# Four banks for transposes, attention as columns, and another split of the single rows in a gather, attention and pooling kernel

## The chip, the cores and the metric

The kernel runs on one NeuronCore of a Trainium2 chip. The metric is the device time of one execution in microseconds (us). The kernel before takes 13519.97 us, the median of 3 runs (13496.62 to 13551.33). One more execution was profiled; the numbers of the profile are its own.

The engines of a core work side by side, each through its own queue of instructions in order: TensorE (PE, with PEld for its weight loads), VectorE (DVE), ScalarE (ACT), GpSimd (POOL) and SyncE (SP, here only a queue for DMAs). They wait for each other by semaphores. PE writes its results into PSUM, which has eight banks of 2 KB in each partition.

## The reference

The inputs are 16384 users with 69 fields each (an index into a table of 100001 rows of 96 float32), and one label index each. In short:

```python
u   = emb[batch_user]                        # 16384 x 69 x 96
ql  = emb[batch_label[:, 0]]                 # 16384 x 96
z   = concatenate([q, u, q - u, q * u])      # q is ql for every field
h   = dice(z @ W1 + b1)                      # 64 wide
att = (h @ W2 + b2) @ W3 + b3                # one number per user and field
pre = where(batch_user < ITEM_NUM, u * att, 0)
pooled = einsum('gf,bfe->bge', window, pre)  # 69 fields into 10 groups
x   = concatenate([pooled, ql])              # 1056 wide
h   = dice(bn(x @ Wf1 + bf1))                # 200
h   = dice(bn(h @ Wf2 + bf2))                # 80
out = h @ Wf3 + bf3                          # 1
```

`dice(x)` is `(alpha * (1 - p) + p) * x` with `p = sigmoid(bn(x))`. The 1.13 million rows of the gather, each of 384 bytes, are the bulk of the data. W1 is split so that `z @ W1` becomes `u @ (W1u - W1qu) + (q * u) @ Wp` and a part that depends on q alone.

## The kernel before, in words

**Tiling.** The batch is cut into 32 blocks of 512 users. A block has 69 chunks of 512 rows: 64 main chunks hold 8 users with their first 64 fields, and 5 tail chunks hold one of the last five fields for all 512 users. Main chunks are pooled by matmuls with window weights; tail chunks go, scaled by their attention, straight into the first layer of the top network with weights prepared for them (`V`). `chunk_of` (L64) numbers the chunks; in all blocks but the last one the five tail chunks come at the end of a block. A step handles two chunks, so there are 1104 steps (`NPAIR`).

**The way of a step.** `fetch` (L361) gathers: each chunk is four tiles of 128 rows, and one `indirect_dma_start` on POOL fetches one tile into the buffer `u` (L268). PE turns each tile into the PSUM tile `ptr`, and DVE copies `ptr` to `uT` (L378) and multiplies it by q into `quT` (L381). `ptr` has two banks. Two steps later `hidden` (L391) computes `ph` from `uT` and `quT` (L401, L405), and ACT computes the sigmoid `y` (L407). A step after that `product` forms the gated value on DVE (L414, L415). `attend_rows` does the attention of four steps at once: PE multiplies the 32-column weights `v2` with y, 32 output rows for each step (`prow`, L421), ACT copies these to the row tile `row` (L423), and a step later `turn_band` transposes it (`patt`, L438), so that each field's attention stands in a partition of its own. `weigh` (L448) makes from it the pooling weights `rw` of four steps. Nine steps after the fetch (`POOL_LAG`) `pool_sums` multiplies `u` by `rw` into one of three sets of `acc` (all three in one bank), and a step later `pool_copy` copies the set into `pooled` on DVE (L489). `u` has 17 buffers, and a gather into a buffer waits until the sums that read it are done.

**Single rows.** Of some chunks the fourth tile is not gathered by POOL. Its 128 rows are fetched one by one by plain DMAs from SP's or ACT's queue (`Singles`, L303), each with an address that the queue has loaded into registers, into a ring of buffers. SP does this for one tile in every 10 steps (109 tiles, 4 buffers), ACT for one in every 8 (136 tiles, 3 buffers), 16 rows in each step, between its own sigmoids. PE waits for these rows on a semaphore of their own.

**The rest.** At a block's end, eight quarter pieces of the top network's first layer (`top1`), then `top2` and `top3`, follow one per step. At a block's start `head_gather` fetches the rows of the labels, `head_turn` transposes them and `head_rows` computes q's part of the hidden layer. The last block has an order of its own, in which the top network runs for quarters of the block.

**What sets the order.** The order on each engine is written out: `plan` holds a list of pieces for each step, and they are emitted step by step under a manual schedule. In the order of a step stand: attention (every fourth step), tail attention, `hidden`, the single rows of ACT, `pool_sums`, `product`, `pool_copy`, `fetch`, `weigh`. The waits between engines are put in by the framework from the tiles that the instructions share; PSUM is guarded by bank.

Of the kernel before, what the change touches and what calls it, by code (L numbers as in the profile page):

```python
# [11 lines left out]
F32 = mybir.dt.float32  # L12
I32 = mybir.dt.int32
# [5 lines left out]
P = 128  # L19
# [21 lines left out]
POOL_LAG = 9  # L41
# [5 lines left out]
CLOSE = 8  # L47

# [3 lines left out]
SP_CHUNKS = [2 * (10 * s + 8) + 1 for s in range(109)]  # L52
SP_RING = 4
ACT_CHUNKS = [2 * (8 * s + 11) for s in range(136)]
ACT_RING = 3
ACT_ROWS = 16
# [6 lines left out]

def chunk_of(c):  # L64

    n, k = divmod(c, NCH)
    if n == NBLK - 1 and k >= EARLY:
        k = NMAIN + k - EARLY if k < EARLY + NTAIL else k - NTAIL
    return n, k
# [47 lines left out]
def rec_kernel(  # L117
# [132 lines left out]
    ps_tr = ctx.enter_context(tc.tile_pool(name="ps_tr", bufs=2, space=PSUM))  # L250
    ps_h = ctx.enter_context(tc.tile_pool(name="ps_h", bufs=2, space=PSUM))
    ps_x = ctx.enter_context(tc.tile_pool(name="ps_x", bufs=2, space=PSUM))
    ps_acc = ctx.enter_context(tc.tile_pool(name="ps_acc", bufs=1, space=PSUM))
    acc = ps_acc.tile([E, 3, 2, NS, G], F32, tag="acc", name="acc")
    ps_m = ctx.enter_context(tc.tile_pool(name="ps_m", bufs=1, space=PSUM))


# [9 lines left out]
    def gather(table, dst, index):  # L267
        nc.gpsimd.indirect_dma_start(  # L268
            out=dst,
            out_offset=None,  # L270
            in_=table,
            in_offset=bass.IndirectOffsetOnAxis(ap=index, axis=0),
        )
# [42 lines left out]

    def single(c, t):
        return places.get(c) if t == SLOT else None
# [5 lines left out]
    def read_rows(op, out, u, c, t, other, **how):  # L324

        at = single(c, t)
        ins = op(out, ring[:, at[0]].bitcast(F32) if at else u[:, 4 * (c % 2) + t, :], other, **how)  # L327
        if at:
            tc.declare_no_dep(ins.ins, group=f"ring{at[0]}", reason="waited for by semaphore")

# [13 lines left out]
    def head_rows(n):  # L344

        for h in range(2):
# [14 lines left out]
    def fetch(i, between=None):  # L361
# [4 lines left out]
        for j in range(2):  # L366
# [3 lines left out]
            ptr = ps_tr.tile([E, 512], F32, tag="tr", name=f"ptr{i}_{j}")  # L370
            for t in range(4):
                if single(2 * i + j, t):
                    wait_for_single(2 * i + j, t)
                else:
                    gather(rows, u[:, 4 * j + t, :], ids[n][:, 4 * k + t : 4 * k + t + 1])
                read_rows(nc.tensor.transpose, ptr[:, t * P : (t + 1) * P], u, 2 * i + j, t, ident)
# [40 lines left out]
    def attend_rows(b, n):  # L417

        pr = ps_x.tile([P, 512], F32, tag="x", name=f"prow{b}")[0 : 32 * n]
        for k in range(n):  # L420
            nc.tensor.matmul(pr[32 * k : 32 * (k + 1), :], v2, ys[b + k], start=True, stop=True)  # L421
        row = rpool.tile([P, 512], F32, tag="row", name=f"row{b}")[0 : 32 * n]
        nc.scalar.copy(row, pr)  # L423
        bands[b] = row
# [8 lines left out]
    def turn_band(b, n):  # L433

        row = bands.pop(b)
        pt = ps_x.tile([P, 4, n, 32], F32, tag="x", name=f"patt{b}")
        for t in range(4):
            nc.tensor.transpose(  # L438
                pt[:, t].rearrange("p k j -> p (k j)"), row[:, t * P : (t + 1) * P], ident[0 : 32 * n, 0 : 32 * n]
            )  # L440
        turned[b] = pt

    def weigh(b, n):

        pt = turned.pop(b)
# [14 lines left out]
    def pool_sums(i):  # L460
# [6 lines left out]
        pa = acc[:, i % 3]  # L467
# [12 lines left out]
        accs[i] = pa, todo  # L480

# [26 lines left out]
    def top1(n, cols, h, part, p1):  # L508

        if part == 0:  # L510

            banks, tag = (ps_h, "h") if n == NBLK - 1 and cols.start >= BLK // 2 and h == 1 else (ps_m, "m")
# [14 lines left out]
    def top2(n, cols):  # L527
        x2 = xpool.tile([D2, BLK], F32, tag="x2", name=f"x2_{n}_{cols.start}")[:, cols]
        g2 = xpool.tile([DH, BLK], F32, tag="g1", name=f"g2_{n}_{cols.start}")[0:D2, cols]
        p2 = ps_m.tile([D2, BLK], F32, tag="m", name=f"p2_{n}_{cols.start}")[:, cols]  # L530
# [5 lines left out]
    def top3(n, cols, x2):  # L536
        k0, k1 = cols.start // P, cols.stop // P
        p3 = ps_m.tile([P, k1 - k0], F32, tag="m", name=f"p3_{n}_{cols.start}")
# [4 lines left out]
    def store(n):  # L543

        p4 = ps_x.tile([n, P], F32, tag="x", name="p4")
# [5 lines left out]
    def top3_last(x2):  # L551

        p3 = ps_m.tile([1, P], F32, tag="m", name="p3_last")
# [5 lines left out]
    pooled, pres, x1s, x2s, qs, us, hs, ys, bands, rws, p1s, gates, turned, accs = ({} for _ in range(14))  # L559

    def top_steps(n, cols):


        def half(h, part):
            if n not in x1s:
                x1s[n] = xpool.tile([DH, 2, BLK], F32, tag="x1", name=f"x1_{n}")
            p1s[n] = top1(n, cols, h, part, p1s.get(n))
# [9 lines left out]
    def rows_of(b, n):  # L577
        return lambda: attend_rows(b, n)

    def spread_of(b, n):  # L580
        def work():
            turn_band(b, n)
            weigh(b, n)

        return work
# [72 lines left out]
    e = c - CLOSE  # L658
    for i in range(e):
        if i >= 7 and i % 4 == 3 and i < e - 1:  # L660
            at(i, rows_of(i - 7, 4))
        if i >= 4:
            at(i, tails_of(i - 4))
        if i >= 8 and i % 4 == 0:
            at(i, lambda b=i - 8: turn_band(b, 4))
# [3 lines left out]
        pools = [] if i < POOL_LAG else [i - POOL_LAG]  # L669
        if i == e - 2:  # L670
            pools.append(i - POOL_LAG + 1)
        elif i == e - 1:
            pools = [i - POOL_LAG + 1]
        at(i, *[lambda k=k: pool_sums(k) for k in pools])
        if i >= 3:
            at(i, product_of(i - 3))
        at(i, *[lambda k=k: pool_copy(k) for k in ([] if i <= POOL_LAG else [i - POOL_LAG - 1, i - POOL_LAG][: 1 + (i == e - 1)])])
        if i == e - 2:
            at(i, rows_of(c - 16, 4))
        elif i == e - 1:  # L680
            at(i, lambda: turn_band(c - 16, 4))
        at(i, fetch_of(i))
        if i >= 8 and i % 4 == 0:
            at(i, lambda b=i - 8: weigh(b, 4))
        elif i == e - 1:
            at(i, lambda: weigh(c - 16, 4))

    at(e, product_of(e - 3), lambda: pool_copy(e - POOL_LAG), tails_of(e - 4))
    for i in range(e, c):
        if (i - 3) % 4 == 3:  # L690
            at(i, rows_of(i - 6, 4))
        at(i, tails_of(i - 3))
        if (i - 4) % 4 == 3:
            at(i, spread_of(i - 7, 4))
        at(i, hidden_of(i - 2), lambda i=i: scalar_rows(i))
        for k in {0: (-16, -15), 1: (-14,), 2: (-13,), 3: (-12, -11), 4: (-10, -9), 7: (-8, -7)}.get(i - e, ()):
            at(i, pool_of(c + k))
        at(i, fetch_of(i))

    at(c, pool_of(c - 6), pool_of(c - 5), tails_of(c - 3), hidden_of(c - 2), fetch_of(c))  # L700
    at(c + 1, tails_of(c - 2), hidden_of(c - 1), fetch_of(c + 1))
    at(c + 2, rows_of(c - 4, 4), tails_of(c - 1), hidden_of(c), spread_of(c - 4, 4), pool_of(c - 4), fetch_of(c + 2))
    at(c + 3, pool_of(c - 3), pool_of(c - 2), hidden_of(c + 1), fetch_of(c + 3, [hidden_of(c + 2)]))
    at(c + 4, pool_of(c - 1), fetch_of(c + 4, [hidden_of(c + 3)]))
    at(c + 5, rows_of(c, 4), spread_of(c, 4), pool_of(c), fetch_of(c + 5, [hidden_of(c + 4)]))
    at(c + 6, pool_of(c + 1), pool_of(c + 2), fetch_of(c + 6, [hidden_of(c + 5)]))
    at(c + 7, pool_of(c + 3), rows_of(c + 4, 2), fetch_of(c + 7, [spread_of(c + 4, 2), hidden_of(c + 6)]))

    for n in range(NBLK):
        first, end = n * NCH // 2, ((n + 1) * NCH - 1) // 2  # L710
        if n > 0:
            if n % NIDS == 1:
                at(max(0, first - 50), lambda n=n: load_ids(n))
            at(first - 14, lambda n=n: qs.__setitem__(n, head_gather(n)))
            at(first - 11, lambda n=n: head_turn(n, qs.pop(n)))
            at(first - 9, lambda n=n: head_rows(n))
        if n < NBLK - 2:
            for s, work in enumerate(top_steps(n, slice(0, BLK))):
# [96 lines left out]
```

## Time and profile before

| | |
|---|---|
| median of 3 runs | 13519.97 us |
| the profiled execution | 13684.32 us |
| its span | 13682.6 us |
| mean clock that TensorE was granted | 0.72 |
| instructions | 171148 |
| PE busy | 9106.3 us (67%) |
| DVE busy | 5074.9 us (37%) |
| ACT busy | 990.6 us (7%) |
| POOL busy | 8225.3 us (60%) |
| gathers of u | 8587, mean 944 ns |
| single rows from ACT's queue and SP's | 17408 and 13952 |

In a line of the costliest groups stand the line of the kernel, the engine, the operation, what it writes and reads by the program's names with partitions x elements, the count, then busy time in us and mean ns of one, and after the bar the idle time of the engine ahead of it with what ended most of it. "Issue" means that the engine waited for nothing that the profile shows. In the list of waits stand the engine, the tile and line that waited, what released it, then the sum in us, how often and the longest.

### The profile page before, as it was taken

To read this page: it belongs to the slowest core of one execution; us is meant where nothing else is said; L and a number is where in the kernel's file an instruction comes from. 1 tells how busy PE (TensorE), PEld (TensorE's weight loads), DVE (VectorE), ACT (ScalarE), POOL (GpSimd) and SP (SyncE) were. 2 spreads that over 40 slices of the span, in tenths; PEclk is the share of its full clock that TensorE was granted. 3 is DMA by queue.
4 is the path that set the end of the run, shared out by engine and by line. 5 is a ranking of instruction groups with operands and counts; after the bars stand their busy time and mean duration, and the time that the engine had idled before them with its cause. 6 is when DMAs were issued, how large, how long until landed. Compare 5 with 4: busy or idle time off the path is not lost.

```text
span 13682.6 us, 171148 instructions
## 1 busy us (share of the span) xinstructions
PE 9106.3 (67%) x41797; PEld 4711.6 (34%) x41797; DVE 5074.9 (37%) x8639; ACT 990.6 (7%) x1657; POOL 8225.3 (60%) x8721
## 2 busy tenths in 40 slices
PE   3666666666666666666776666666666666676668
PEld 1333333333333333333333333333333333333334
DVE  2333333333333333333333333333333333333333
ACT  0000000000000000000000000000000000000001
POOL 5666566656666656666665665665665666556663
PEclk7677776777767777677776777777777777777677
DMA  1111111111111111111111111111111111111111
GB/s 38 34 34 33 34 33 33 33 35 33 33 34 34 35 33 33 33 33 36 33 33 33 33 36 33 34 33 33 36 33 33 34 33 35 33 33 34 33 33 22
DMA packets 344459, 458.45 MB, mean 34 GB/s; under 512 B 202354, under 2 KB 202866, under 8 KB 343330
## 3 DMA queue, kind: packets, MB, share of 16 engines
q0 software_dynamic: 278880, 428.92, 15.0%
q1 hardware_dynamic: 29762, 11.82, 0.4%
q10 hardware_dynamic: 34816, 6.75, 0.3%
q8 instruction: 336, 5.51, 0.2%
q14 instruction: 665, 5.45, 0.1%
HBM read 446.74 MB, written 0.07 MB: 33 GB/s over the span
## 4 chain that ended last, share of the span: by engine, by line
PE 37%; issue 20%; another core or an unknown queue 18%; ACTq 12%; DVE 10%; POOL 2%; ACT 1%; DMA 0%; POOLq 0%
ACTq L303 10%; PE acc L327 8%; PE ph L401 6%; PE ptr L327 6%; PE ph L405 5%; PE p L521 5%; DVE uT L378 3%; DVE quT L381 2%; POOL u L268 2%; PE prow L421 2%; DVE y L415 1%; DVE y L414 1%; ACTq L288 1%; PE pa L430 1%
## 5 line engine op out<-in xcount | busy, mean ns | idle before, releaser
L268 POOL DMA_INDIRECT u<-in_rows,ids x8587 | 8103.5, 944 | 5290.9 <-issue 2228.3
L327 PE MATMUL acc<-rw,u 128*96 128x20 f32 x15930 | 1972.9, 269 | 1685.7 <-issue 1088.5
L489 DVE COPY pooled<-acc 96x160 f32<-96x160 f32 x1008 | 429.0, 426 | 6575.4 <-remote 4728.2
L327 PEld LDWEIGHTS acc<-rw,u 128*96 128x96 f32 x15930 | 1853.6, 201 | 2757.0 <-issue 1954.3
L327 PE MATMUL ptr<-ident,u 128*96 128x128 f32 x8587 | 1655.6, 341 | 866.1 <-issue 659.3
L378 DVE COPY uT<-ptr 96x512 f32<-96x512 f32 x2208 | 1485.9, 673 | 996.2 <-remote 756.4
L405 PE MATMUL ph<-quT,wn 96*64 96x512 f32 x4416 | 1625.1, 727 | 195.2 <-issue 189.6
L401 PE MATMUL ph<-uT,A 128*64 128x512 f32 x4096 | 1637.7, 830 | 156.9 <-issue 106.2
L327 PEld LDWEIGHTS ptr<-ident,u 128*96 128x96 f32 x8587 | 1250.6, 166 | 1082.2 <-issue 864.1
L381 DVE TENSOR_TENSOR quT<-ptr,qT 96x512 f32<-96x512 f32 x2048 | 1378.6, 673 | 0.0
L407 ACT ACTIVATE y<-ph 128x512 f32<-128x512 f32 x1104 | 658.6, 597 | 8853.1 <-remote 3304.5
L405 PEld LDWEIGHTS ph<-quT,wn 96*64 96x64 f32 x4416 | 447.3, 175 | 1257.0 <-issue 1255.2
L414 DVE SCALAR_TENSOR_TENSOR y<-y,na1c,ph 128x512 f32<-128x512 f32 x1104 | 810.3, 734 | 177.1 <-ACT y L407 97.0
L415 DVE SCALAR_TENSOR_TENSOR y<-ph,wn,y 128x512 f32<-128x512 f32 x1104 | 828.8, 751 | 39.4
L521 PE MATMUL p<-pooled,wf 96*100 96x512 f32 (+1 forms) x1400 | 713.8, 643 | 84.9 <-issue 82.0
L438 PE MATMUL patt<-ident,row 128*128 128x128 f32 x1108 | 259.5, 375 | 641.4 <-issue 274.9
L421 PE MATMUL prow<-y,v 128*32 128x512 f32 x2208 | 540.7, 851 | 115.0 <-issue 95.6
L401 PEld LDWEIGHTS ph<-uT,A 128*64 128x64 f32 x4096 | 279.0, 169 | 868.9 <-issue 783.3
L521 PE MATMUL p<-pre,V 96*100 96x512 f32 (+1 forms) x700 | 424.0, 745 | 140.4 <-issue 89.2
L438 PEld LDWEIGHTS patt<-ident,row 128*128 128x128 f32 x1108 | 185.1, 194 | 775.8 <-issue 554.0
L521 PEld LDWEIGHTS p<-pooled,wf 96*100 96x100 f32 x1400 | 251.0, 192 | 450.3 <-issue 450.0
L430 PE MATMUL pa<-y,vrep 64*96 64x512 f32 x320 | 231.3, 895 | 203.2 <-DVE pre L431 127.6
(72 smaller groups left out, 2682.1 us busy)
## 6 DMA issues: line engine op xcount, KB each, us to landing
ring<-in_rows ACTq DMA_DIRECT2D x17408, 0.4 KB
ring<-in_rows SPq DMA_DIRECT2D x13952, 0.4 KB
u<-in_rows,ids POOLq DMA_INDIRECT x8587
ids<-in_idx SPq DMA_DIRECT2D x8, 560.0 KB, 2.5
q<-in_emb,ids POOLq DMA_INDIRECT x128
wf<-in_far SPq DMA_DIRECT2D x1, 1209.0 KB
wn<-in_near SPq DMA_DIRECT2D x1, 236.0 KB, 3.1
ids<-in_idx SPq DMA_DIRECT2D x1, 140.0 KB
```

The source lines that it names most:

```text
L268: nc.gpsimd.indirect_dma_start(out=dst, out_offset=None, in_=table, in_offset=bass.IndirectOffsetOnAxis(ap=index, axis=0),)
L303: d = self.engine.dma_start(out=ring[r : r + 1, b], in_=row_bytes[:, bass.ds(self.values[r], ROW_BYTES)]).then_inc(self.sems[k], 16)
L327: ins = op(out, ring[:, at[0]].bitcast(F32) if at else u[:, 4 * (c % 2) + t, :], other, **how)
L378: nc.vector.tensor_copy(uT[j][0:E], ptr)
L381: nc.vector.tensor_tensor(quT[:, j, :].rearrange("e (s f) -> e s f", f=FM), ptr.rearrange("e (s f) -> e s f", f=FM), by_field(q[:, k * NS ...
L401: nc.tensor.matmul(p, As[n % 2][:, k // 4, :], uT[j], start=True, stop=False)
L405: nc.tensor.matmul(p, Wp, quT[:, j, :], start=False, stop=True)
L407: nc.scalar.activation(y, ph, AF.Sigmoid, scale=S_DICE)
L414: nc.vector.scalar_tensor_tensor(y, y, na1c, ph, ALU.mult, ALU.mult)
L415: nc.vector.scalar_tensor_tensor(y, ph, a1c, y, ALU.mult, ALU.add)
L421: nc.tensor.matmul(pr[32 * k : 32 * (k + 1), :], v2, ys[b + k], start=True, stop=True)
L521: nc.tensor.matmul(p1, w[:, h * DH : (h + 1) * DH], x, start=(k == 0), stop=(k == KTOP - 1))
```

## The change

- `ptr` has four banks, not two. To make room, `ps_x` has one bank instead of two, and the bank `ps_m` is gone: the first two layers of the top network use `ps_x`, and `top3` a corner of the bank that holds the sums.
- In `fetch` the four gathers of a tile's chunk are emitted first, then the four transposes. The first transpose is made to wait for all of them by a dependency added by hand, and of the four only the first waits and only the last signals.
- Attention becomes columns: `attend` does one step at a time with four matmuls, in which a 128-column piece of y is the weight and two columns of `v2` move. Its result has the layout that `weigh` wants, and `attend_rows`, its copy on ACT and `turn_band` are gone. The result lies in the bank of the sums (`shared`), which keeps two sets of sums instead of three, and five places for the attention of four steps.
- `POOL_LAG` is 10, and the sums of a step now stand after `attend` and after `pool_copy` of the sums before.
- The five tail chunks of a block stand at the chunks 48, 53, 58, 63 and 68 (`TAIL_AT`).
- SP fetches a tile of single rows in every 8 steps (136 tiles), ACT one in every 11 (98 tiles), 12 rows in each step.
- `mark`, after the sums of every fourth step, increments a semaphore from PE's queue, and then drains PE with an increment of a second one. Nothing waits for either.
- The pieces at a block's start and end, and the end of the program, have other steps.

```diff
-POOL_LAG = 9
+POOL_LAG = 10
+QUARTERS = [
+    [-12, -12, -11, -11, -10, -10, -9, -9, -8, -7],
+    [-5, -5, -5, -4, -3, -3, -3, -2, -1, 0],
+    [3, 3, 3, 4, 5, 5, 5, 6, 7],
+]
...
-SP_CHUNKS = [2 * (10 * s + 8) + 1 for s in range(109)]
+SP_CHUNKS = [2 * (8 * s + 8) + 1 for s in range(136)]
-ACT_CHUNKS = [2 * (8 * s + 11) for s in range(136)]
+ACT_CHUNKS = [2 * (11 * s + 14) for s in range(98)]
-ACT_ROWS = 16
+ACT_ROWS = 12
...
+TAIL_AT = [48 + 5 * f for f in range(NTAIL)]
...
-    if n == NBLK - 1 and k >= EARLY:
-        k = NMAIN + k - EARLY if k < EARLY + NTAIL else k - NTAIL
+    if n == NBLK - 1:
+        if k >= EARLY:
+            k = NMAIN + k - EARLY if k < EARLY + NTAIL else k - NTAIL
+    elif k in TAIL_AT:
+        k = NMAIN + TAIL_AT.index(k)
+    else:
+        k -= sum(at < k for at in TAIL_AT)
...
-    ps_tr = ctx.enter_context(tc.tile_pool(name="ps_tr", bufs=2, space=PSUM))
+    ps_tr = ctx.enter_context(tc.tile_pool(name="ps_tr", bufs=4, space=PSUM))
-    ps_x = ctx.enter_context(tc.tile_pool(name="ps_x", bufs=2, space=PSUM))
+    ps_x = ctx.enter_context(tc.tile_pool(name="ps_x", bufs=1, space=PSUM))
-    acc = ps_acc.tile([E, 3, 2, NS, G], F32, tag="acc", name="acc")
-    ps_m = ctx.enter_context(tc.tile_pool(name="ps_m", bufs=1, space=PSUM))
+    shared = ps_acc.tile([P, 512], F32, tag="shared", name="shared")
+    sets = shared[0:E, 0:320].rearrange("e (k j s g) -> e k j s g", k=2, j=2, g=G)
+
+    def place(b, n):
+        start = 320 + 32 * (b // 4 % 5) + 8 * (b % 4)
+        return shared[:, start : start + 8 * n].rearrange("p (t k j) -> p t k j", t=4, j=2)
...
+    marks = [tc.alloc_semaphore(f"mark{k}") for k in range(2)]
+
+    def mark():
+        nc.tensor.sem_inc(marks[0], 1)
+        nc.tensor.drain().then_inc(marks[1], 1)
...
+            come = []
             for t in range(4):
                 if single(2 * i + j, t):
                     wait_for_single(2 * i + j, t)
                 else:
-                    gather(rows, u[:, 4 * j + t, :], ids[n][:, 4 * k + t : 4 * k + t + 1])
-                read_rows(nc.tensor.transpose, ptr[:, t * P : (t + 1) * P], u, 2 * i + j, t, ident)
+                    come.append(gather(rows, u[:, 4 * j + t, :], ids[n][:, 4 * k + t : 4 * k + t + 1]))
+            for t in range(4):
+                ins = read_rows(nc.tensor.transpose, ptr[:, t * P : (t + 1) * P], u, 2 * i + j, t, ident)
+                for g in come if t == 0 else []:
+                    tc.add_manual_dep(ins.ins, g.ins.name, DATA)
...
-    def attend_rows(b, n):
-        pr = ps_x.tile([P, 512], F32, tag="x", name=f"prow{b}")[0 : 32 * n]
-        for k in range(n):
-            nc.tensor.matmul(pr[32 * k : 32 * (k + 1), :], v2, ys[b + k], start=True, stop=True)
-        row = rpool.tile([P, 512], F32, tag="row", name=f"row{b}")[0 : 32 * n]
-        nc.scalar.copy(row, pr)
-        bands[b] = row
+    def attend(i, b, n):
+        out = place(b, n)
+        for t in range(4):
+            nc.tensor.matmul(out[:, t, i - b, :], ys[i][:, t * P : (t + 1) * P], v2[:, 0:2], start=True, stop=True)
...
-    def turn_band(b, n):
...
     def weigh(b, n):
-        pt = turned.pop(b)
+        pt = place(b, n)
...
-        pa = acc[:, i % 3]
+        pa = sets[:, i % 2]
...
         accs[i] = pa, todo
+        if i % 4 == 0:
+            mark()
...
-    for i in range(e):
-        if i >= 7 and i % 4 == 3 and i < e - 1:
-            at(i, rows_of(i - 7, 4))
+    for i in range(c - 12):
         if i >= 4:
             at(i, tails_of(i - 4))
-        if i >= 8 and i % 4 == 0:
-            at(i, lambda b=i - 8: turn_band(b, 4))
         if i >= 2:
             at(i, sums_of(i - 2))
         at(i, lambda i=i: scalar_rows(i))
...
+        for k in [i - 5] if i < f else [i - 5, i - 4] if i == f else [i - 4]:
+            if k >= 0:
+                at(i, lambda k=k: attend(k, k - k % 4, 4) if k < f - 8 else attend(k, k - k % 2, 2))
         if i >= 3:
             at(i, product_of(i - 3))
+        pools = range(pooled_to, max(pooled_to, i - (POOL_LAG if i < f else max(7, POOL_LAG - 1 - (i - f) // 6)) + 1))
+        at(i, *[lambda k=k: pool_copy(k) for k in copies] if i else [])
+        at(i, *[lambda k=k: pool_sums(k) for k in pools])
...
         at(i, fetch_of(i))
-        if i >= 8 and i % 4 == 0:
-            at(i, lambda b=i - 8: weigh(b, 4))
+        if i < f and i >= 9 and (i - 9) % 4 == 0:
+            at(i, lambda b=i - 9: weigh(b, 4))
...
-            at(first - 14, lambda n=n: qs.__setitem__(n, head_gather(n)))
-            at(first - 11, lambda n=n: head_turn(n, qs.pop(n)))
-            at(first - 9, lambda n=n: head_rows(n))
+            at(first - 16, lambda n=n: qs.__setitem__(n, head_gather(n)))
+            at(first - 13, lambda n=n: head_turn(n, qs.pop(n)))
+            at(first - 11, lambda n=n: head_rows(n, [0]))
+            at(first - 9, lambda n=n: head_rows(n, [1]))
+        steps = [12, 12, 13, 13, 15, 15, 16, 16, 18, 20] if n < NBLK - 2 else [8, 8, 9, 9, 10, 10, 11, 11, 12, 13]
```

## The prediction

> **What bounds the kernel now.** I read the page first (busy shares, chain, costliest groups), then all waits, then timelines of POOL, DVE and SP. Busy shares and chain:
>
> ```profile
> PE 9106.3 (67%) x41797; PEld 4711.6 (34%) x41797; DVE 5074.9 (37%) x8639; ACT 990.6 (7%) x1657; POOL 8225.3 (60%) x8721
> PE 37%; issue 20%; another core or an unknown queue 18%; ACTq 12%; DVE 10%; POOL 2%; ACT 1%; DMA 0%; POOLq 0%
> ACTq L303 10%; PE acc L327 8%; PE ph L401 6%; PE ptr L327 6%; PE ph L405 5%; PE p L521 5%; DVE uT L378 3%; DVE quT L381 2%; POOL u L268 2%; PE prow L421 2%; DVE y L415 1%; DVE y L414 1%; ACTq L288 1%; PE pa L430 1%
> ```
>
> No engine is full; the chain passes between them, and its largest line is ACT's queue issuing single rows. 1104 steps of two chunks make 12.39 us a step; PE works 8.25 of it. A timeline of POOL (start, duration, idle before):
>
> ```profile
> 6157.13 0.95 POOL L268 DMA_INDIRECT u<-in_rows,ids  x1 [0.30 <-issue]
> 6158.39 0.94 POOL L268 DMA_INDIRECT u<-in_rows,ids  x1 [0.30 <-issue]
> 6159.64 0.94 POOL L268 DMA_INDIRECT u<-in_rows,ids  x1 [0.30 <-issue]
> 6162.86 0.94 POOL L268 DMA_INDIRECT u<-in_rows,ids  x1 [2.27 <-remote]
> ```
>
> Gathers come every 1.245 us, 0.30 of it ended by no wait. 8715 of them (8587 of u, 128 of q) are 10,850 us: POOL's floor, 9.8 us a step. The other 2,830 us are pauses. Sorting POOL's gaps in the trace: 886 of 1.5 to 4 us, mean 2.5, mostly after 7 or 8 gathers, so about one a step; 42 of 4 to 8; 36 longer (495 us), nearly all at block ends (about 12 us each).
>
> POOL waits for the sums of eight steps earlier, which free u. Why are they late?
>
> ```profile
> DVE pooled L489 <- remote: 4728.2, 578, 28.5
> ACT y L407 <- issue: 2600.7, 274, 20.9
> POOL u L268 <- remote: 1517.4, 610, 6.1
> ```
>
> "Remote" is a release without a visible end of an instruction. Two timelines from the start, where POOL gathers unbroken until 175 us, DVE and SP's queue:
>
> ```profile
> 90.84 0.69 DVE L378 COPY uT<-ptr 96x512 f32<-96x512 f32 x1 [9.85 <-remote]
> 102.16 0.69 DVE L378 COPY uT<-ptr 96x512 f32<-96x512 f32 x1 [10.03 <-remote]
> 113.47 0.69 DVE L378 COPY uT<-ptr 96x512 f32<-96x512 f32 x1 [10.03 <-remote]
> ```
>
> ```profile
> 31.85 114.66 SPq L303 DMA_DIRECT2D ring<-in_rows  x41
> 189.56 60.92 SPq L303 DMA_DIRECT2D ring<-in_rows  x116
> ```
>
> Each copy awaits four transposes of 1.06 us together, yet copies stand 11.3 us apart: four signals, 2.8 us each. SP's rows too come every 114.66/41 = 2.8 us, but every 0.53 us after 189 us, where POOL mostly stands. Setting all 11,358 PE signals against their matmuls' ends: 70% post over 1 us late, 90% of those from 3 us into a run of gathers on; with POOL standing, 34 ns apart. And rows by POOL's phase: SP issues 1.4 to 2.9 a us in the first 3 us of a run, 0.5 to 1.1 later, 0.4 to 0.7 until 1.5 us after its end, then 2.5 to 3. So signals and row queues live on POOL's pauses, and each step takes one: that is the bound, more than any engine.
>
> ACT feels it most. Between its sigmoids (12.30 us) the 16 rows of a step take 9.96 us, and in 66% of the steps the sigmoid starts within 0.8 us of the last row: rows hold it up, behind it wait product, sums and POOL.
>
> **What the Trainium skill says.** "TensorE: Matmul & The Clock Gate", The cost: per-tile semaphore tail: increments at completion serialize, about 26 ns each; one on the last matmul is enough. The trace agrees while POOL stands (34 ns), not while it gathers (2.8 us): the measurement decides. "PSUM — Partial Sum Buffer", PSUM bank collisions: guard by bank and quadrant, not by address; so attention and sums in one bank wait for each other. Its Engine vs sequencer instructions: a drain waits until the engine is wholly idle; the trace of before has none in its loop.
>
> **The change part by part**, against the profiled 13684 us.
>
> *ACT's rows and copies.* 98 tiles, not 136: 12,544 rows, 28% fewer; 11.4 a step, 7.1 us for 9.96. The chain's ACTq 12% is 1,640 us; 28% of it is -460. The 275 row copies (160.5 us) go with it. Bounds 0 (if POOL's pause sets the step anyway) and -1,640. I take -460.
>
> *SP's rows.* 136 tiles, not 109: 15.8 rows a step, not 12.6. SP is free of waits for its ring 85% of the time and then takes 0.81 us a row. ACT in the same phases takes 0.65. At 0.81 a tile needs 104 us, at 0.65 83 us, and eight steps are 99 us now. I take the middle, 0.73: 93.4 us, a floor of 11.7 us a step, under the forecast: 0. Upper bound: the third rival's price.
>
> *Signals.* Per step 11,358/1104 = 10.3 before (8 from transposes), 6,025/1104 = 5.5 after, counted in the programs. Bounds: 0, and pauses in the share of signals that 9.8 us of gathers don't let through at 2.8 us (6.8 of 10.3 before, 2.0 of 5.5 after): 886 x 0.55 left, 399 fewer by 2.2 = -880. The rows still need a pause a step, so I shorten pauses rather than drop them: to 2.25 us, 886 x 0.25 = -220.
>
> *Four transpose banks.* Transposes wait for gathers and PE's own past, no longer for DVE. The sums ahead of them still wait for DVE: 0 alone, part of the -220.
>
> *Attention as columns.* Out go prow (540.7 us) and patt (259.5): 0.72 us of PE a step. In come four matmuls with 128 weight columns, two records each as f32. Nearest row: acc, 16 records in 1.53 us warm or 2.75 cold; eight by 128/96 are 1.0 to 1.8 us. Net +0.3 to +1.1, hidden by PE's 4.1 us of idle; uncovered +330 to +1,200. I take 0.
>
> *The shared bank.* Each step now has PE attention, DVE's copy of the last sums, PE's next sums, back to back; before, a step's other matmuls lay between. Behind the waiting sums stand transposes and hidden matmuls, and DVE, ACT and POOL behind these. Bounds: 0, and copy and sums (0.42 + 1.53) on each pause, +1,730. I take the copy: 886 x 0.42 = +370.
>
> *Tail chunks spread.* The five chunks without sums stand five apart, not together. 31 block ends at 12 us: bounds 0 and -370; half, -185.
>
> *Look-ahead* of seven steps, not eight: 69 us of gathers still outlast several pauses: 0. q gathers and head matmuls start two steps earlier, the same ones: 0.
>
> *Gathers.* 234 single tiles, not 245: 11 x 1.245 = +14.
>
> *Unread signals.* 275 drains between sums and transposes; nothing reads them. No row shows one; the fill of one group, 0 to 1 us: 0 to +275, or below nothing if a drain frees held signals (bounded by the -880). I take +100. Some 2,200 more waits in PE's queue at 0 to 0.7 us, its pace under gathers: hidden by PE's idle, else +1,540.
>
> *End.* From 13,500 us on PE works 153 of 182 us; a new order gives 0 to -29: 0.
>
> Sum: -460 - 220 + 370 - 185 + 14 + 100 = -381. The profiled run stood 164 us over the median, which I keep: 13,520 - 380 = 13,140.
>
> **The rivals.**
> *Pauses go with the signals*: -880 for -220: 12,480. For it: 53 runs of 16 gathers ended in one such pause. Against: a queue issues 0.4 to 0.5 rows a us past 10 us of a run, and needs 16 a step. No pauses at all, 10,864 + 300, is out for this reason. 12,300 to 12,800, chance 0.15.
> *Nothing moves*: the pause is POOL's own and merely hides ACT; -460 and -220 go, +370 is hidden too: 13,400 to 13,600. For it: pauses are alike, 2.2 us, after 7, 8 and 16 gathers. Chance 0.15.
> *Slower: SP's rows bound.* At 0.81 us a row, 15.8 rows need 12.8 us a step: 14,130 profiled, 13,970 at the median; with fewer ACT rows beside it SP may gain 10%. It decides from 128 rows above eight steps (0.77 us a row now). For it: SP's rates by phase give 14 rows in a run of 9.8 and a pause of 2.2. Against: a late tile makes a pause, in which rows take 0.4. 13,600 to 14,300, chance 0.25.
> *It doesn't do what it says*: signals don't trickle one by one, so halving them does nothing: within the second.
>
> **How the numbers follow.** Likeliest, 0.45: 13,140, on its own 12,850 to 13,420 (ACT's or the bank's term off by two thirds). The 8 in 10 range reaches over most of the first and third rivals: 12,350 to 14,050. Within 0.5%, about what a measurement can tell from no change (13,452 to 13,588), lie two thirds of the second: 0.10. Slower: the third and 0.01: 0.26. Faster: 0.45 + 0.15 + 0.04 = 0.64.
>
> **What would show it.** Right: about one POOL gap over 1.5 us a step still, but shorter; ACT's waits ended by issue far under 2600.7 us, chain's ACTq under 6%; uT copies at the start under 6 us apart; block ends near 6 us; sums waiting for the pooled copy up from 77.1 us. Wrong: SP busy without ring waits and transposes waiting for its rows (third rival); 450 gaps (first); 900 unchanged ones (second). The prediction fails if rows, not signals, set the pause.

## The result, and the profile after

The changed kernel takes 14547.04 us (median of 4 runs, 14521.68 to 14578.23), the kernel before beside it 13512.31 us: 1.0762 times as long, with a 95% interval of 1.073 to 1.0794. The forecast was 13,140 us, in a range of 12,350 to 14,050.

The profiled execution of the changed kernel has a span of 14552.0 us, 869 us more than the profiled one of before. The latter, 13,684 us long, stood above the median beside the changed kernel, so the 869 us are less than the 1,035 us between the medians; a pair from one chip follows below. The page's busy shares and its chain:

```profile
PE 10791.9 (74%) x47313; PEld 6704.6 (46%) x47313; DVE 5217.5 (36%) x8725; ACT 848.5 (6%) x1380; POOL 8258.1 (57%) x8732
PE 53%; another core or an unknown queue 17%; DVE 15%; issue 14%; ACT 1%; ACTq 1%; POOL 0%; DMA 0%; POOLq 0%
PE shared L354 16%; PE ptr L354 11%; PE ph L433 7%; PE ph L437 6%; PE shared L453 5%; DVE uT L410 4%; PE p L542 4%; DVE quT L413 3%; DVE y L447 2%; DVE y L446 2%; PE pa L459 2%; DVE pooled L510 1%; PE ph L430 1%; DVE rw L467 1%
```

ACT's queue, which held 12% of the chain before, holds 1%, as the change intends. In its place PE went from 37% to 53%, with the sums in the shared bank (L354) first and attention's columns (L453) further on. The waits of the changed kernel that answer to those shown of before (engine, tile and line; what released it; us in all, times, longest):

```profile
DVE uT L410 <- PE ptr L354: 3694.4, 891, 12.2
POOL u L288 <- PE shared L354: 2830.6, 603, 61.4
DVE pooled L510 <- remote: 2243.8, 425, 13.7
PE shared L354 <- DVE pooled L510: 1146.1, 391, 12.5
ACT y L439 <- issue: 3149.9, 281, 25.9
```

The fourth line is the new one: sums waiting for the copy cost 77.1 us before. The last one went the wrong way: the forecast took ACT's waits ended by issue for the work of its rows and saw them fall far below 2600.7 us. POOL's waits, of which the largest group was "remote" before, are now mostly for sums that had just ended. Following each wait to the end of the matmul that it was for says the same. Before, POOL's pauses (all of its gaps longer than the usual 0.30 us) came to 2970 us, and in 2075 of these the awaited matmul had ended already and only its signal was late. After, they come to 3773 us, of which 1086 are late signals. So the time in which POOL waited for sums that PE had not yet finished rose from 895 to 2687 us, while the late signals of the sums themselves cost half of what they did.

One step shows how. These are PE and POOL in two timelines of the changed kernel (start, duration, idle before), and the copy between them from DVE's:

```profile
6027.86 1.05 PE L453 MATMUL shared<-v,y 128*128 128x2 f32 x8
6041.39 2.75 PE L354 MATMUL shared<-rw,u 128*96 128x20 f32 x16 [12.48 <-DVE pooled L510]
6043.98 1.92 PE L354 MATMUL ptr<-ident,u 128*96 128x128 f32 x8
```

```profile
6040.92 0.42 DVE L510 COPY pooled<-shared 96x160 f32<-96x160 f32 x1 [5.84 <-remote]
```

```profile
6037.77 0.96 POOL L288 DMA_INDIRECT u<-in_rows,ids  x1 [0.30 <-issue]
6044.42 0.95 POOL L288 DMA_INDIRECT u<-in_rows,ids  x1 [5.69 <-PE shared L354]
```

Attention ends at 6028.91, in a run of gathers. The copy must wait for its signal, because both touch one bank, and the copy starts only at 6040.92, 2.2 us after POOL stopped. Until then PE stands, since the sums come after the copy. Only now do they run, 2.75 us long, and POOL waits for them: its pause is 5.69 us, not some 2.3 as in the prediction's timeline. So sums that are late on PE are late because another signal was held a link earlier. Sorted, POOL's gaps over 1.5 us are these (e5 and e6 are both kernels again, on one chip):

| gaps of POOL (profiled run) | 1.5 to 4 us | 4 to 8 us | over 8 us |
|---|---|---|---|
| before | 886, 2242 us | 42, 217 us | 36, 495 us |
| after | 673, 1573 us | 353, 1962 us | 22, 248 us |
| before, e5 | 883, 2216 us | 40, 213 us | 39, 517 us |
| after, e6 | 629, 1554 us | 420, 2315 us | 13, 175 us |

The middle column grew by 1745 us, the others shrank by 916: together +829 of the 869 us. On the one chip of e5 and e6 it grew by 2102 us and the others shrank by 1004: +1098 of 1134 us.

### The profile page after: what moved, and what is told of

Its sections match the earlier page's. It is cut to its first block, busy times and chain, and to the rows that moved or that the text cites. A ratio compares the mean times of both kernels' runs of the same rounds, so it can differ in the third digit from the quotient of the medians.

```text
span 14552.0 us, 181666 instructions
## 1 busy us (share of the span) xinstructions
PE 10791.9 (74%) x47313; PEld 6704.6 (46%) x47313; DVE 5217.5 (36%) x8725; ACT 848.5 (6%) x1380; POOL 8258.1 (57%) x8732
## 4 chain that ended last, share of the span: by engine, by line
PE 53%; another core or an unknown queue 17%; DVE 15%; issue 14%; ACT 1%; ACTq 1%; POOL 0%; DMA 0%; POOLq 0%
PE shared L354 16%; PE ptr L354 11%; PE ph L433 7%; PE ph L437 6%; PE shared L453 5%; DVE uT L410 4%; PE p L542 4%; DVE quT L413 3%; DVE y L447 2%; DVE y L446 2%; PE pa L459 2%; DVE pooled L510 1%; PE ph L430 1%; DVE rw L467 1%
## 5 line engine op out<-in xcount | busy, mean ns | idle before, releaser
L354 PE MATMUL shared<-rw,u 128*96 128x20 f32 x15954 | 2497.2, 309 | 2682.8 <-issue 1367.7
L354 PEld LDWEIGHTS shared<-rw,u 128*96 128x96 f32 x15954 | 2370.1, 251 | 2779.8 <-issue 1422.9
L354 PE MATMUL ptr<-ident,u 128*96 128x128 f32 x8598 | 2036.3, 413 | 491.5 <-remote 394.2
L433 PE MATMUL ph<-uT,A 128*64 128x512 f32 x4096 | 1955.3, 974 | 152.1 <-DVE y L447 96.6
L453 PEld LDWEIGHTS shared<-v,y 128*128 128x128 f32 x8832 | 1229.5, 215 | 1560.9 <-issue 1113.1
L354 PEld LDWEIGHTS ptr<-ident,u 128*96 128x96 f32 x8598 | 1618.6, 203 | 586.1 <-remote 412.4
L437 PE MATMUL ph<-quT,wn 96*64 96x512 f32 x4416 | 1746.0, 792 | 0.0
L453 PE MATMUL shared<-v,y 128*128 128x2 f32 x8832 | 1322.1, 272 | 358.9 <-DVE rw L467 255.4
L510 DVE COPY pooled<-shared 96x160 f32<-96x160 f32 x946 | 397.6, 421 | 3084.6 <-remote 2243.8
L446 DVE SCALAR_TENSOR_TENSOR y<-y,na1c,ph 128x512 f32<-128x512 f32 x1104 | 810.7, 734 | 86.2 <-ACT y L439 77.1
L430 PE MATMUL ph<-qT,Cq 97*64 97x512 f32 x320 | 297.1, 1040 | 0.0
```

The costliest lines, as they stand in the source:

```text
L433: nc.tensor.matmul(p, As[n % 2][:, k // 4, :], uT[j], start=True, stop=False)
L437: nc.tensor.matmul(p, Wp, quT[:, j, :], start=False, stop=True)
L446: nc.vector.scalar_tensor_tensor(y, y, na1c, ph, ALU.mult, ALU.mult)
L453: nc.tensor.matmul(out[:, t, i - b, :], ys[i][:, t * P : (t + 1) * P], v2[:, 0:2], start=True, stop=True)
```

## The experiments

Letters in the expectations: H, the round trip from attention to the copy to the sums through the shared bank is the loss; W, PE's added work is; D, the drains are; R, SP's rows are; S, fewer signals are a gain that something hides. The runs met different chips, so each is read by its ratio to the kernel before on its own chip. The changed kernel's own ratio differs between chips, 1.0762 and 1.0772 where the kernel before takes 13,510 us and 1.0869 where it takes 13,654; a difference of about 0.01 or less between runs of two chips is therefore not clear of the chips.

| run | edit | time, us | before there, us | ratio (95%) |
|---|---|---|---|---|
| e1 | after, copy ahead of attention | 11033.35 | 10953.04 | 1.0073 (1.0056 to 1.009) |
| e2 | after, no marks | 11028.97 | 10953.04 | 1.0072 (1.0055 to 1.0089) |
| e3 | after, old split of rows | 11041.33 | 10953.04 | 1.0083 (1.0067 to 1.01) |
| e4 | after, each transpose waits and signals | 11028.21 | 10953.04 | 1.007 (1.0054 to 1.0087) |
| e5 | before | 13675.33 | 13653.92 | 1.0016, one run |
| e6 | after | 14838.77 | 13653.92 | 1.0869 (1.0844 to 1.0894) |
| e7 | after, attention in its own bank | 13687.36 | 13653.92 | 1.0028 (1.0018 to 1.0039) |
| e8 | before, one of four transposes waits and signals | 13679.21 | 13653.92 | 1.0014 (1.0 to 1.0027) |
| e9 | after, copy ahead of attention | 13799.06 | 13688.23 | 1.008 (1.0063 to 1.0096) |
| e10 | before, 98 tiles on ACT | 13582.51 | 13688.23 | 0.9921 (0.9905 to 0.9938) |
| e11 | after, no marks | 14642.36 | 13688.23 | 1.0694 (1.0676 to 1.0712) |
| e12 | e7 with the old split of rows | 13736.03 | 13688.23 | 1.0028 (1.0015 to 1.0041) |
| e13 | after | 14561.69 | 13508.02 | 1.0772 (1.0753 to 1.079) |
| e14 | e7 without marks | 13484.47 | 13508.02 | 0.9978 (0.9969 to 0.9986) |
| e15 | before, tails spread | 13265.88 | 13508.02 | 0.9823 (0.9806 to 0.9839) |
| e16 | before, 67 tiles on ACT | 13379.77 | 13508.02 | 0.9908 (0.9891 to 0.9925) |
| e17 | e15 and e16 together | 13294.77 | 13665.66 | 0.9726 (0.971 to 0.9742) |
| e18 | e14 with 18 buffers of u | 13598.7 | 13665.66 | 0.9944 (0.9927 to 0.996) |

**e1 to e4: a chip without the hold.** Each undoes one thing in the changed kernel. The first:

```diff
-        for k in [i - 5] if i < f else [i - 5, i - 4] if i == f else [i - 4]:
-            if k >= 0:
-                at(i, lambda k=k: attend(k, k - k % 4, 4) if k < f - 8 else attend(k, k - k % 2, 2))
         if i >= 3:
             at(i, product_of(i - 3))
...
         at(i, *[lambda k=k: pool_copy(k) for k in copies] if i else [])
+        for k in [i - 5] if i < f else [i - 5, i - 4] if i == f else [i - 4]:
+            if k >= 0:
+                at(i, lambda k=k: attend(k, k - k % 4, 4) if k < f - 8 else attend(k, k - k % 2, 2))
         at(i, *[lambda k=k: pool_sums(k) for k in pools])
```

> The changed kernel with one thing moved: in the steps of the main loop the DVE copy of the last sums is emitted ahead of the attention matmuls, not behind them. The same instructions run on PE in the same order; only the waits differ: the copy no longer waits for attention, attention waits for the copy. Theory H (the round trip attention - copy - sums in the shared bank is what made the changed kernel slower): the sums' waits for the pooled copy (1289 us in the changed kernel) all but go, POOL's 353 gaps of 4 to 8 us become few, and the time comes to 13,300 to 13,700. Theory W (PE's added work: attention's 8832 records and weight loads, at a lower clock): the same work remains, 14,300 to 14,600. Theory D (the drains): no change either, 14,450 to 14,600.

The second leaves out the calls of `mark`:

```diff
-        if i % 4 == 0:
-            mark()
```

> The changed kernel without the semaphore increments and drains that nothing reads. Theory D (each of 275 drains empties PE and lets the held signals pile up): 100 to 900 us faster. Theories H and W: within 100 us of the changed kernel, 14,450 to 14,600.

The third restores the split of the single rows:

```diff
-SP_CHUNKS = [2 * (8 * s + 8) + 1 for s in range(136)]
+SP_CHUNKS = [2 * (10 * s + 8) + 1 for s in range(109)]
-ACT_CHUNKS = [2 * (11 * s + 14) for s in range(98)]
+ACT_CHUNKS = [2 * (8 * s + 11) for s in range(136)]
-ACT_ROWS = 12
+ACT_ROWS = 16
```

> The changed kernel with the single rows split as before: 109 tiles from SP's queue, 136 from ACT's, 16 rows in a step. Theory R (128 rows in eight steps are too many for SP's queue): SP gets slack and the time falls to 13,700 to 14,100. Theories H and W: SP is not what is waited for (the trace of the changed kernel shows it standing for its ring a quarter of the time), so ACT's queue, again busy with 16 rows a step, costs something: 14,500 to 14,900.

The fourth restores the old loop of `fetch`:

```diff
-                    come.append(gather(rows, u[:, 4 * j + t, :], ids[n][:, 4 * k + t : 4 * k + t + 1]))
-            for t in range(4):
-                ins = read_rows(nc.tensor.transpose, ptr[:, t * P : (t + 1) * P], u, 2 * i + j, t, ident)
-                for g in come if t == 0 else []:
-                    tc.add_manual_dep(ins.ins, g.ins.name, DATA)
+                    gather(rows, u[:, 4 * j + t, :], ids[n][:, 4 * k + t : 4 * k + t + 1])
+                read_rows(nc.tensor.transpose, ptr[:, t * P : (t + 1) * P], u, 2 * i + j, t, ident)
```

> The changed kernel with gathers and transposes emitted in turn as before, so that each transpose waits for its own gather and all four signal. Theory S (fewer signals are the gain of the change, hidden under a loss elsewhere): 300 to 900 us slower than the changed kernel, 14,850 to 15,450, with DVE's idle before the pooled copy growing again. If waiting at the first transpose for all of four gathers is itself what costs: up to 300 us faster.

Every expectation in microseconds was missed, since the kernel before itself takes 10,953 us on this chip. All four lie within 14 us of each other, so here none of the disputed parts matters (the changed kernel itself was not run there). Two lines of e1's trace show why: POOL's largest group of waits, with the longest one at its end, and SP's queue at the start:

```profile
POOL u L288 <- issue: 2440.6, 7997, 0.3
```

```profile
31.98 118.22 SPq L323 DMA_DIRECT2D ring<-in_rows  x299
```

After the first gather no wait of POOL is longer than 0.3 us: 8726 gathers run end to end, 1.25 us apart without one pause. And SP issues 299 rows in 118.22 us while POOL gathers without a break (2.5 a us), against 41 in 114.66 in the profile before. Signals come at once too: four transposes of the start end at 71.77 us, and DVE's copy that waits for them starts at 71.81. Gathers are as long here (946 ns), but they hold up neither rows nor signals. The experiments that could decide had to be run on chips where they do.

**e5 to e8: where gathers hold up signals.** e5 is the kernel before, for its trace.

> The kernel before, unchanged, for its trace beside those of the other runs of this call. The first four runs met a chip on which it takes 10,953 us, not 13,512. If POOL's pauses are the whole difference, its trace there shows gathers 1.245 us apart without any gap over 1 us, signals posted within 0.1 us of the matmul's end, and some 10,950 us; where it takes about 13,500 us, one pause a step as in the profile before.

It has the pauses, one in nearly every step (table above).

> The changed kernel, unchanged. Where the kernel before takes about 13,500 us: 14,450 to 14,650. Where it takes about 10,950 us, POOL's gathers are the bound, and the change can only add its eleven gathers (14 us) and what it does to the start and the end: 10,960 to 11,050.

The ratio is 1.0869, somewhat more than 1.0762, and the time is 189 us above the upper end of the expectation. The loss itself is there, with 420 gaps of 4 to 8 us.

e7 takes attention out of the sums' bank, and one bank from the transposes for it:

```diff
-    ps_tr = ctx.enter_context(tc.tile_pool(name="ps_tr", bufs=4, space=PSUM))
+    ps_tr = ctx.enter_context(tc.tile_pool(name="ps_tr", bufs=3, space=PSUM))
...
+    ps_att = ctx.enter_context(tc.tile_pool(name="ps_att", bufs=1, space=PSUM))
+    columns = ps_att.tile([P, 512], F32, tag="columns", name="columns")
...
-        return shared[:, start : start + 8 * n].rearrange("p (t k j) -> p t k j", t=4, j=2)
+        return columns[:, start : start + 8 * n].rearrange("p (t k j) -> p t k j", t=4, j=2)
```

> The changed kernel with attention's columns in a bank of their own, and three banks for the transposes, so that neither the copy of the sums waits for attention nor attention for the copy. Where gathers hold up signals, theory H (the round trip in the shared bank): 13,300 to 13,900; theory W (PE's added work): 14,300 to 14,600. Where they don't: no change against the changed kernel (within 30 us), but the sums' waits for the pooled copy shrink from about 600 us to under 150.

Of the 1185 us that e6 lost, 1151 are gone, as theory H expected. The same matmuls run, so theory W falls as the main cause. So does the clock granted to TensorE, another candidate: it was 0.72 in the kernel before and 0.66 in e6, and it is 0.67 here. One step of e7, PE and DVE:

```profile
6031.84 1.87 PE L455 MATMUL columns<-v,y 128*128 128x2 f32 x8
6036.08 1.47 PE L356 MATMUL shared<-rw,u 128*96 128x20 f32 x8 [2.38 <-issue]
```

```profile
6035.62 0.41 DVE L512 COPY pooled<-shared 96x160 f32<-96x160 f32 x1
6043.67 0.69 DVE L412 COPY uT<-ptr 96x512 f32<-96x512 f32 x1 [7.64 <-remote]
```

The copy at 6035.62 has no idle time ahead of it: it stands in line behind DVE's other work and waits for no signal of attention. The sums follow within the run of gathers, and POOL's next pause is 2.19 us. The waits of e7's sums for the copy:

```profile
PE shared L356 <- DVE pooled L512: 180.6, 98, 14.7
```

They were 1295.6 us in e6 and are 180.6 here; the gaps of 4 to 8 us fall from 420 to 67. What remains is one pause of about 2.4 us in nearly every step (979 gaps, 2345 us), as in the kernel before.

e8 puts the new loop of `fetch`, shown with e4, into the kernel before.

> The kernel before with one part of the change alone: gathers of a chunk first, then its four transposes, of which the first waits for all and the last signals. Where gathers hold up signals, theory S (a step's pause is as long as its signals need): 300 to 900 us faster than the kernel before; if the pause is set by rows or by the round trip: within 100 us of it. Where they don't: within 30 us of it.

The time differs by 25 us, with an interval that begins at 1.0. Theory S falls for the loop as the change has it: six signals fewer in a step, together with the wait of the first transpose for all four gathers, neither shorten the pause nor make it rarer (879 gaps, 2193 us). The two halves of the edit were not tried apart.

**e9: the other way out of the round trip.** The kernel of e1 again, with all else of the changed kernel, four transpose banks and the shared bank included.

> The changed kernel with the copy of the last sums emitted ahead of the attention matmuls, as in e1, once more, for a chip where gathers hold up signals. Theory H: the shared bank costs because the copy waits for a signal of matmuls that end just ahead of it; turned round, the copy waits for nothing new, attention waits for a copy that can be done long before, and the time is that of e7 (own bank, 1.003 of before): ratio 1.00 to 1.03. If any use of one bank by both costs (waits in either order): 1.06 to 1.09, as the changed kernel. Where gathers hold up nothing: 1.005 to 1.009, as e1.

The ratio is 1.008, as H says, and the sums hardly wait for the copy any more:

```profile
PE shared L354 <- DVE pooled L510: 10.9, 10, 2.1
```

POOL has 60 gaps of 4 to 8 us. Only the order of two pieces on two engines differs from the changed kernel, and some 7 to 8% of the time goes with it; even e11, which has less to do on PE, takes 843 us longer on the same chip. The bank may be shared, if the copy doesn't stand behind matmuls whose signal is held. e7 and e9 remove the same thing in two ways: both cut the link from attention to the copy. The other link, the sums behind the copy, stays in both; in the kernel before the sums stood ahead of the copy, and that order was not tried with the shared bank.

**e10, e12, e16: rows.** e10 and e16 take tiles from ACT's queue in the kernel before and give them to POOL; e10 uses the new 98 tiles and 12 rows, e16 this:

```diff
-ACT_CHUNKS = [2 * (8 * s + 11) for s in range(136)]
+ACT_CHUNKS = [2 * (16 * s + 19) for s in range(67)]
-ACT_ROWS = 16
+ACT_ROWS = 8
```

> The kernel before with 98 tiles from ACT's queue in place of 136, 12 rows in a step, all else as it was (SP keeps its 109): POOL gathers 38 tiles more, +47 us. The prediction's step on ACT (rows hold up the sigmoid and through it the step, -460 us): ratio 0.965 to 0.975. If POOL's pause sets the step and hides ACT's rows: 1.002 to 1.006. Where gathers hold up nothing: 1.004.

The result lies between the two expectations: -106 us, or -153 if the 47 us of added gathers are taken out. ACT's rows hold something up, but it is worth a third of what the chain's share suggested.

> The kernel before with 67 tiles from ACT's queue (one in every 16 steps, 8 rows in a step), not 136: POOL gathers 69 tiles more, +86 us. With 98 tiles the ratio was 0.992. If rows on ACT set part of each pause in proportion: another -1%, 0.980 to 0.986. If 98 tiles already take ACT out of the way, only the gathers are left: 0.994 to 0.996.

This is -128 us, or -214 without the added gathers (ratio 0.9908), again between the two expectations. The second half of the tiles brings less than the first, as far as two chips can be compared.

e12 is e7 with the edit of e3.

> The changed kernel with attention in a bank of its own as in e7, and single rows split as before (109 tiles from SP's queue, 136 from ACT's). In e7 SP's queue issues in 95% of the time. If SP's rows are what is left of the loss there, the ratio falls from 1.003 to 0.97 to 0.99; if the pause is set by PE's signals alone: 1.00 to 1.01; if ACT's rows set it: above 1.01.

The ratio is 1.0028 as in e7, on another chip: the split as a whole moves nothing that can be seen. The edit takes rows from SP and gives more to ACT at once, and ACT's part alone was worth 106 us in the kernel before (e10), so a gain on SP and a loss on ACT could cancel here; no run moves SP's rows alone. For the changed kernel the trace speaks against SP: its queue waits for its ring during 3300 us (1470 in the profile before), and it takes about 0.6 us a row when the ring is free (0.81 before).

**e11, e13, e14: the unread signals.** e11 is the kernel of e2, e13 the changed kernel again, e14 is e7 with the edit of e2.

> The changed kernel without the increments and drains that nothing reads, as in e2, for a chip where gathers hold up signals. Theory D (they cost): ratio to before at least 0.02 under the changed kernel's 1.087. Otherwise 1.08 to 1.09; if the drains help held signals out, above 1.10.

> The changed kernel, unchanged, beside the other runs of this call; its ratio to before has been 1.076 and 1.087. On the chip of e11 (1.069 without the unread signals) the marks' cost is the difference. If they cost what the prediction took (+100 us): 1.077. If nothing: 1.068 to 1.071.

> The changed kernel with attention in a bank of its own and without the unread signals. With marks it stood at 1.0028 of before on two chips. If a drain costs some 0.4 us on the path of the pause (275 times): 0.994 to 0.997. If the drains fall into time that PE has anyway: 1.001 to 1.004.

Without marks the ratio is 1.0694, with them 1.0772 and 1.0869 on two other chips; in the own-bank version it is 0.9978 against 1.0028. By the smallest two of these differences that is 0.5 to 0.8%, 70 to 105 us. e11 and e14 both lie between their expectations, and no two runs with and without marks met the same chip, so the size isn't shown. That the drains hold PE up is: the Trainium skill ("PSUM — Partial Sum Buffer", Engine vs sequencer instructions) says that a drain waits until the engine is idle, and the trace agrees. In the changed kernel transposes wait on "remote" in this line:

```profile
PE ptr L354 <- remote: 394.2, 130, 8.3
```

Each of these 130 waits ends 0.3 us after a drain does, and e11's trace has none of them. How much of the 394 us reaches the end of the program is open.

**e15: tail chunks.** `chunk_of` and `TAIL_AT` of the change, in the kernel before.

> The kernel before with one part of the change: the five tail chunks of a block stand at the chunks 48, 53, 58, 63 and 68, not in a row at its end. Prediction: block ends cost about half, -185 us, ratio 0.984 to 0.989. If the long pause at a block's end only moves or splits into short ones: 0.998 to 1.002.

This is -242 us, more than expected. Gaps over 8 us fall from 36 in the profile before to 16, and from 495 to 205 us.

**e17 and e18: what adds up.** e17 joins e15 and e16.

> The kernel before with the tail chunks spread as in e15 and 67 tiles from ACT's queue as in e16, nothing else of the change. If both terms add up: 0.982 x 0.991 = 0.973 (0.970 to 0.977). If the tails' gain was ACT's relief at block ends under another name: 0.980 to 0.984.

The ratio of 0.9726 is the product of both ratios (0.9733) within its interval. This version is 371 us faster than the kernel before on the same chip, and so faster than both kernels.

e18 is e14 with one buffer more:

```diff
-    upool = ctx.enter_context(tc.tile_pool(name="upool", bufs=17))
+    upool = ctx.enter_context(tc.tile_pool(name="upool", bufs=18))
```

> The changed kernel with attention in a bank of its own, without the unread signals (e14, 0.998) and with 18 buffers of u for 17, so that gathers run eight steps ahead again, as before. If the look-ahead of seven is what costs 1.6% there: 0.980 to 0.986. If it is PE's added work and waits in the loop: 0.995 to 0.999.

The ratio is 0.9944, just below the second expectation: the shorter look-ahead may cost some 0.3%, but e14 ran on another chip, so this isn't shown; the greater part of the 1.6% between e14 and e15 has another cause.

## Why the prediction was wrong

**The step that failed** is "The shared bank". It named the mechanism and what stands behind the waiting sums, and it gave bounds of 0 and +1,730 us; it took +370, the copy's 0.42 us on each pause. Measured are 1151 us (e6 less e7). The mis-sized term left out what the prediction itself had found first: a signal posted in a run of gathers comes late, and attention's signal is such a one. That the two wait for each other at all is what the Trainium skill's rule ("PSUM — Partial Sum Buffer", PSUM bank collisions: guard by bank and quadrant) makes of a shared bank, and the trace agrees: the copy of columns 0 to 319 waited for matmuls that write from column 320 on. The pause therefore has to hold the signal, the copy and the sums, the upper bound, in 353 of the pauses, and PE stands idle until then, so that it cannot use the time of the gathers to do the sums ahead. Taking the upper bound alone would have given 14,500. Of the 1,407 us by which the forecast was too low, some 780 are this term; most of the rest are two gains that did not come, most of the 460 us of ACT's rows and the 220 of the signals.

**Signals.** -220 taken, about 0 measured (e8). The step rested on a price of 2.8 us per signal, read from four signals in 11.3 us. The changed kernel posts one signal for four transposes, and its copies at the start stand as far apart:

```profile
84.82 0.69 DVE L410 COPY uT<-ptr 96x512 f32<-96x512 f32 x1 [9.91 <-remote]
95.32 0.69 DVE L410 COPY uT<-ptr 96x512 f32<-96x512 f32 x1 [9.22 <-issue]
```

They stand 10.5 us apart here and 11.2 us apart at 129.65 and 140.85, where under 6 was forecast. What is held is held for as long with a quarter of the signals. The prediction had this as its last rival, that signals don't trickle one by one; these copies and e8 bear out its mechanism, though not the time that it gave.

**ACT's rows.** The term was right in sign in the kernel before: -460 taken, and alone the rows give -106 with their gathers (e10). The likely reason, not shown by itself, is that a chain's share is what lies on one path of many that end nearly together; when 28% of it goes, the next path sets the pause. In the changed kernel ACT's queue did fall from 12% to 1% of the chain, but its waits ended by issue rose, and with the split put back the own-bank version takes as long (e12).

**SP's rows.** The prediction took 0; no run moves them alone, and the split as a whole measures 0 in the own-bank version (e12). The slower rival, which had a chance of 0.25 and pointed in the right direction, is not the mechanism of the loss: in the changed kernel SP waits for its ring longer than before, and moving attention alone removes the loss with SP's rows unchanged (e7). That rival came nearest to the measured time by luck.

**Tail chunks.** -185 taken, -242 measured (e15): right. **Unread signals.** +100 taken, 70 to 105 by the smallest differences between chips: right in sign, the size not shown. **Look-ahead.** 0 taken, perhaps 46 (0.34%, e18 against e14).

**What stays open.** Without the round trip the change is worth +34 us (e7, 13,687 less 13,654). The terms, as far as they are measured, are -242 for tails, some +68 for marks, some +46 for the look-ahead and 0 for the split and the signals, -128 in all; so about 160 us are not accounted for, in a sum that joins several chips. Attention's columns on PE are one candidate: in e7 their records take 1382 us and their weight loads 1289, against 800 us for the matmuls of the old way and 262 for its loads. The lower clock granted to TensorE, 0.67 for 0.72, is another, and the two may go together. No run has tried them alone, and the prediction's 0 for them is neither shown nor refuted. Whether fewer signals and the new waits give something once attention stands elsewhere was not tried either. What sets the one pause of about 2.4 us that nearly every step keeps on these chips once the round trip is gone is not shown: neither fewer signals (e8) nor the split (e12) removed it. Four transpose banks were not tried alone either; e7 with three and e9 with four lie 0.5% apart, on two chips.

**The range.** It ended at 14,050. The shared bank's upper bound was kept inside the likeliest case and not made a case of its own. As a rival with the price of +1,730 it would have reached over the result.

## What to carry to other kernels

Before two engines' tiles move into one PSUM bank, write down the order of their pieces on both engines: a copy that stands behind freshly issued matmuls waits for their signal, one that stands ahead of them waits for nothing new, and here that order alone was worth 7 to 8% on chips where signals are held. Where a trace shows signals arriving late, price each new round trip with the whole lateness and with the work that can't be done meanwhile, not with the copy's own duration. A rate such as "2.8 us a signal" needs a second case with another count before a sum rests on it.

## What the runs showed of the hardware

The kernel before takes 10,953 us on one chip and 13,508 to 13,688 us on four others, with gathers of 944 to 946 ns on all of them. The difference goes with what POOL's gathers do to other queues. In the traces of the four chips rows and PE's signals get through slowly while POOL gathers and quickly some 1.5 to 2 us after it stops; in those of the one chip (e1 to e4) they are not held and POOL never pauses. The sizes agree: e5's pauses, less 0.30 us for each, come to 2,670 us, and the two times differ by 2,722 us. On the one chip the four variants of the changed kernel lie at 1.007 to 1.008 of the kernel before, and none of the disputed edits makes a difference. The prediction's limit of a run without pauses, 10,864 us and the end, is near the time there. The kernel before has no trace on that chip, and what distinguishes the chips the runs don't show.
